# Interleaving the groups of an MLP's first layer with a lag of two parts

## The chip, the core and the metric

The kernel runs on one core of a Trainium2 chip. The metric is device time in microseconds for one execution, the median of several runs. Five engines work side by side: TensorE (PE in the profile) does the matmuls into PSUM banks, VectorE (DVE) and ScalarE (ACT) do elementwise work and empty PSUM, GpSimd (POOL) does elementwise work on SBUF, and SyncE (SP) issues the DMAs. Each engine executes its own list of instructions in order, and a wait at the head of the list holds everything behind it.

## The reference

Eight batches of x (100 rows of 512 numbers) attend to a context of 361 rows. A first plain cross-attention adds alpha times its result to x. Two multi-head cross-attentions with 16 heads of width 128 follow, each behind a layer norm and with biases and one extra bias key. The last stage is an MLP, and it is the only stage that the change touches:

```python
h = _layer_norm(x, ln_mlp_scale, ln_mlp_offset)
h = jax.nn.gelu(h @ w_fc1 + b_fc1, approximate=False) @ w_fc2 + b_fc2
return x + h
```

w_fc1 is 512 by 2048 and w_fc2 is 2048 by 512. Everything is float32.

## The kernel before

The MLP runs twice, for the batches 0 to 3 (half 0) and 4 to 7 (half 1). In each half the transposed activations are four chunks of 128 features by 400 rows. Both layers multiply with a fast scheme on 2 by 2 blocks that needs seven block products in place of eight, at the price of sums of blocks made beforehand.

The first layer of a half is cut into four groups, k = 0 to 3, of 512 hidden features each. `hidden_sums` (L1027) forms the sums of a group's weight blocks with four additions on POOL (helper `left_sums`, L1007 to L1010). `hidden_in` (L1016) forms the sums of the activations on DVE (helper `right_sums`, L1001 to L1004), once per half. `hidden` (L1034) then does a group in four parts, each with two products but the last, which has one:

- part 0: product gx (A11·B11), copied by ACT to c11 (L1058); product gy (A12·B21), added to c11 by DVE (L1059); gelu on ACT (L1055).
- part 1: product gz (S1·T1), copied by ACT to c22 (L1062); product S2·T2 added onto gx, copied by ACT to c12 (L1063).
- part 2: S4·B22 added onto gz, which DVE adds to c12 (L1065), and gelu; S3·T3 added onto gx, which DVE adds to c22 (L1067), and gelu.
- part 3: A22·T4 added onto gx, gelu straight from PSUM to c21; then the four `right_sums` of the group on DVE, which the second layer reads.

gx and gz gather several products in one PSUM bank each. A product that adds onto such a bank can't start before the engine that read the bank's earlier content is done. So the second product of part 1 waits for the copy of c11, part 2 waits for the copies of part 1, and part 3 waits for DVE's addition to c22.

The second layer follows: `mlp_sums` (L1074) forms the sums of w_fc2's blocks with four additions on DVE, and `mlp_out` (L1082) does its products (pfx, pfy, pfz in the profile). Both layers' weights are loaded by SP in pieces of 512 KB into a ring of six slots (class `Ring`, L51). Each group of the first layer holds two slots. A load into a slot is written behind the last unit that uses the slot's earlier content: group 3 takes the slots of group 0, and the second layer's first four pieces take those of groups 1 and 2. The sums of a group lie in a buffer of two turns (tag pT), so those of group k+2 wait for the last use of group k's, which is in its part 2.

`mlp_units` (L1238) returns the lists of units. The list `hid` of the first layer is written in the order: sums 0, hidden_in, then group after group, with the sums of the next group between parts 1 and 2 of a group. At the end (L1373) the kernel writes hid for half 0, then the second layer woven with the norm of half 1, then hid of half 1 woven with the final transposes and stores of half 0 (list `end`), then the second layer of half 1.

The order written is not yet the order of each engine's list. When the program is built, a planner goes through time with durations of its own and gives an engine that it takes to be free the first instruction, by the order written, that it takes to be ready. The trace shows the lists that came out of it.

Of the kernel before, what the change touches and what calls it, by code (L numbers as in the profile page):

```python
# [80 lines left out]
def two_cross_attentions(ctx: ExitStack, tc: tile.TileContext, a: dict, out: bass.AP):  # L81
# [11 lines left out]
    def psum(pool, shape, name):  # L93
        return pool.tile(shape, F32, tag=pool.name, name=name)
# [110 lines left out]
    def unit(fn, *keys):  # L205
        return fn, keys
# [360 lines left out]
    def normed(n, q, c):  # L567
        if c == 0:
            if n < 2:
                hTs[n, q] = work.tile([P, DT, NQ], F32, tag="hT", name=f"hT_{n}_{q}", bufs=1)  # L570
            elif q % 2 == 0:
                t = cpool.tile([P, 7 * 2 * KH], F32, tag="cT", name=f"hT_{n}_{q}")
                t = t[:, : DT * 2 * NQ].rearrange("p (c n) -> p c n", c=DT)
                for i in range(2):
                    hTs[n, q + i] = t[:, :, i * NQ : (i + 1) * NQ]
                hTs["mlp", q // 2] = t
            for j in range(QB):
                b = q * QB + j
                h = hTs["rows", j] = xs.pop(b)
                nc.vector.tensor_scalar(h, h, mv[:, b, 0:1], rstd[:, b : b + 1], ALU.subtract, ALU.mult)  # L580
        pt = psum(ps_t, [P, NQ], f"ph_{n}_{q}_{c}")
        for j in range(QB):
            nc.tensor.transpose(
                pt[:, j * L : (j + 1) * L], hTs["rows", j][:, c * P : (c + 1) * P], ident[:L, :L]
            )
        nc.vector.tensor_scalar(
            hTs[n, q][:, c, :], pt, vec_b[:, 2 * n, c : c + 1], vec_b[:, 2 * n + 1, c : c + 1], ALU.mult, ALU.add
        )
# [107 lines left out]
    pTs, probs, sums = {}, {}, {}  # L696
# [303 lines left out]
    def right_sums(engine, b11, b12, b21, b22, t1, t2, t4):  # L1000
        engine.tensor_tensor(t1, b12, b11, ALU.subtract)  # L1001
        engine.tensor_tensor(t2, b22, t1, ALU.subtract)
        engine.tensor_tensor(b12, b12, b22, ALU.subtract)
        engine.tensor_tensor(t4, b21, t2, ALU.subtract)  # L1004
# [7 lines left out]
    def blocks_of(t, n):  # L1012

        return [t[:, i * n : (i + 1) * n, j * NQ : (j + 1) * NQ] for i in range(2) for j in range(2)]

    def hidden_in(hf):  # L1016
        h = blocks_of(hTs["mlp", hf], 2)
        t = work.tile([P, 3, 2, NQ], F32, tag="pb", name=f"ht_{hf}", bufs=1)
        right_sums(nc.vector, *h, t[:, 0], t[:, 1], t[:, 2])
        ts["h", hf] = dict(zip(("B11", "T3", "B21", "B22", "T1", "T2", "T4"), h + [t[:, i] for i in range(3)]))  # L1020
        g0, g1 = (of[:, i * 3200 : (i + 1) * 3200].rearrange("p (f t) -> p f t", f=8) for i in range(2))
        t = zf[:, 6400:11200].rearrange("p (u f t) -> p u f t", u=3, f=8)
        g = [x[:, :, j * NQ : (j + 1) * NQ] for x in (g0, g1) for j in range(2)]
        gs[hf] = g
        ts["g", hf] = dict(zip(("B11", "T3", "B21", "B22", "T1", "T2", "T4"), g + [t[:, i] for i in range(3)]))

    def hidden_sums(hf, k):  # L1027
        w1, w2 = w4(("f1", hf, k)), w4(("f1", hf, 4 + k))
        t = work.tile([P, 3, 2, 256], F32, tag="pT", name=f"fs_{hf}_{k}")
        blocks = [w1[:, :2], w1[:, 2:], w2[:, :2], w2[:, 2:]]  # L1030
        left_sums(nc.gpsimd, *blocks, t[:, 0], t[:, 1], t[:, 2])
        ws["h", hf, k] = dict(zip(("A11", "A12", "S3", "A22", "S1", "S2", "S4"), blocks + [t[:, i] for i in range(3)]))

    def hidden(hf, k, part):  # L1034

        a, b = ws["h", hf, k], ts["h", hf]
        c11, c12, c21, c22 = (g[:, 2 * k : 2 * k + 2, :] for g in gs[hf])
        key = "h", hf, k

        def add(name, sa, sb, first=False):  # L1040
            if first:
                mm[key, name] = psum(ps_mm, [P, 2, NQ], f"p{name}_{hf}_{k}")
            ps = mm[key, name]
            for f in range(2):
                for c in range(2):
                    nc.tensor.matmul(  # L1046
                        ps[:, f, :], a[sa][:, c, f * P : (f + 1) * P], b[sb][:, c, :],
                        start=first and f == c == 0, stop=f == c == 1, skip_group_check=True,
                    )
            return ps  # L1050

        def gelu(dst, src, block):
            for f in range(2):
                i = block * 8 + 2 * k + f
                nc.scalar.activation(dst[:, f, :], src[:, f, :], AF.Gelu, bias=vec["b_fc1"][:, i : i + 1])  # L1055

        if part == 0:
            nc.scalar.copy(c11, add("gx", "A11", "B11", True))  # L1058
            nc.vector.tensor_tensor(c11, add("gy", "A12", "B21", True), c11, ALU.add)  # L1059
            gelu(c11, c11, 0)  # L1060
        elif part == 1:
            nc.scalar.copy(c22, add("gz", "S1", "T1", True))  # L1062
            nc.scalar.copy(c12, add("gx", "S2", "T2"))  # L1063
        elif part == 2:
            nc.vector.tensor_tensor(c12, add("gz", "S4", "B22"), c12, ALU.add)  # L1065
            gelu(c12, c12, 0)
            nc.vector.tensor_tensor(c22, add("gx", "S3", "T3"), c22, ALU.add)  # L1067
            gelu(c22, c22, 1)
        else:
            gelu(c21, add("gx", "A22", "T4"), 1)  # L1070
            t = [ts["g", hf][n][:, 2 * k : 2 * k + 2, :] for n in ("T1", "T2", "T4")]
            right_sums(nc.vector, c11, c12, c21, c22, *t)

    def mlp_sums(hf, c):  # L1074
        blocks = [w8(("f2", hf, cc, half)) for cc in (c, c + 2) for half in range(2)]
        t = cpool.tile([P, 20 * P], F32, tag="ctx", name=f"fs1_{hf}_{c}")
        t = t[:, :2048].rearrange("p (u f n) -> p u f n", u=2, f=8)
        s4 = work.tile([P, 8, P], F32, tag="pT", name=f"fs4_{hf}_{c}")
        left_sums(nc.vector, *blocks, t[:, 0], t[:, 1], s4)
        ws["o", hf, c] = dict(zip(("A11", "A12", "S3", "A22", "S1", "S2", "S4"), blocks + [t[:, 0], t[:, 1], s4]))  # L1080
# [119 lines left out]
    def rows_unit(q, tag="h"):  # L1200

        return unit(lambda: [load_rows(q * QB + j, tag=tag) for j in range(QB)])
# [35 lines left out]
    def mlp_units(hf):  # L1238
        norm = []
        for q in (2 * hf, 2 * hf + 1):  # L1240
            norm.append(rows_unit(q, "sums"))
            norm += [unit(lambda q=q, c=c: normed(2, q, c)) for c in range(DT)]
        hid, mlp = [unit(lambda: hidden_in(hf))], []
        for k in range(4):
            keys = [(W, ("f1", hf, k)), (W, ("f1", hf, 4 + k))]
            sums = unit(lambda k=k: hidden_sums(hf, k), *keys)
            hid.insert(len(hid) - 2 if k else 0, sums)
            hid += [unit(lambda k=k, part=part: hidden(hf, k, part), *keys) for part in range(4)]
        for c in range(2):
            a11, a12, a21, a22 = ((W, ("f2", hf, cc, half)) for cc in (c, c + 2) for half in range(2))  # L1250
            mlp.insert(len(mlp) - 1 if c else 0, unit(lambda c=c: mlp_sums(hf, c), a11, a12, a21, a22))
            for part, keys in enumerate(((a11, a12), (), (a21,), (a22,))):
                mlp.append(unit(lambda c=c, part=part: mlp_out(hf, c, part), *keys))
        def ends(j, chunks=range(DT)):
            return unit(lambda: back(ys["mlp", hf], j * L, hf * 4 + j, store, chunks))

        def fetch(*js):
            return unit(lambda: [load_rows(hf * 4 + j, "h" if j < 2 else "sums") for j in js])

        end = [fetch(2, 3), ends(2), ends(3), fetch(0, 1)]  # L1260
        end += [ends(j, cs) for cs in (range(3), range(3, 4)) for j in range(2)]
        return norm, hid, mlp, end
# [49 lines left out]
    for n, (l, q, g) in enumerate(steps):  # L1312
        ahead = project_units(n + 1) if n + 1 < len(steps) else []
        half_ahead = (len(ahead) + 1) // 2
        for j in range(QB):
            fill = []
            k = 2 * g + j
# [6 lines left out]
            part = ahead[:half_ahead] if j == 0 else ahead[half_ahead:]  # L1324
# [7 lines left out]
            part = woven(part, outs) if len(part) > len(outs) else woven(outs, part)  # L1332
            if mix:
# [3 lines left out]
                part = part[lead:]  # L1337
# [17 lines left out]
            lists, k = [], 0  # L1355
            for i, us in enumerate(groups):
                upto = (i + 1) * len(fill) // len(groups)
                lists += [us] + [[u] for u in fill[k:upto]]
                k = upto
            units += apart(lists)  # L1360
    n = len(steps) - 1
    drain = mix_units(n, 1) + [probs_unit(n)] + out_units(n)[1:] + close_units(1, 1)
    norm, hid, mlp, end = mlp_units(0)
    norm1, hid1, mlp1, end1 = mlp_units(1)
    units += held[8:] + norm[:5] + woven(drain, norm[5:])

# [33 lines left out]
```

## Time and profile before

| | us |
|---|---|
| median of 3 runs | 2000.42 (1997.58 to 2003.01) |
| the profiled execution | 2003.46 |
| its span, first to last instruction | 2001.6 |
| PE busy in the span | 1956.1 (98%) |
| DVE busy | 1278.3 (64%) |
| ACT busy | 755.1 (38%) |
| POOL busy | 703.7 (35%) |

PE's clock was granted at 0.999 of full speed over the span. In the trace the first layer of half 0 runs from about 1833 us to 1877 us, the second from there to 1912 us; half 1 follows to about 1960 us and to the end. In the stage of half 0's first layer (1833 to 1877 us) PE was busy 41.29 of 44.00 us, in that of half 1 (1912 to 1960 us) 47.15 of 48.00 us. A float32 matmul appears as two records on PE; one product of the first layer is eight records, and each of them takes about 0.17 us from start to start.

### The profile page before, as it was taken

What the parts mean: (1) busy time and instruction counts of PE and PEld (TensorE: products, weight loads), DVE (VectorE), ACT (ScalarE), POOL (GpSimd) and SP (SyncE); (2) the same over time, 40 slices, a digit from 0 to 9 for tenths busy, and PEclk for the clock granted to TensorE, in tenths of its full rate; (3) what the DMA queues carried; (4) which work ended last, traced back from release to release, by engine and by line L of the source; (5) the groups of instructions that cost most, each with busy time, mean ns of one, the idle gap of its engine ahead of it and who ended that gap; (6) DMA issues with size and microseconds to landing.
All of it is one profiled execution on the core that took longest, in us unless ns stands there. A gap on an engine that the chain in (4) does not pass through costs nothing.

```text
span 2001.6 us, 31490 instructions
## 1 busy us (share of the span) xinstructions
PE 1956.1 (98%) x10991; PEld 1810.4 (90%) x10991; DVE 1278.3 (64%) x3523; ACT 755.1 (38%) x2002; POOL 703.7 (35%) x1147
## 2 busy tenths in 40 slices
PE   9999999999999999999999999999999999999998
PEld 5668899999999899999999899999999999889998
DVE  2564776667677676676765756676767666765543
ACT  1324544344442344344433344444433444321231
POOL 3233433543344144434242323333243243225140
PEclk9999999999999999999999999999999999999999
DMA  7696324742645357616543453234334433135442
GB/s 254 248 318 208 95 83 125 233 137 66 192 155 163 107 143 236 192 54 188 171 128 115 129 172 99 85 88 159 92 123 126 144 119 87 45 97 180 124 126 70
DMA packets 250682, 283.89 MB, mean 142 GB/s; under 512 B 37608, under 2 KB 212108, under 8 KB 247196
## 3 DMA queue, kind: packets, MB, share of 16 engines
q1 hardware_dynamic: 246340, 271.51, 43.5%
q0 software_dynamic: 2112, 6.40, 0.9%
q10 hardware_dynamic: 2072, 3.97, 0.6%
q8 instruction: 88, 1.44, 0.3%
q14 instruction: 70, 0.57, 0.1%
HBM read 242.86 MB, written 38.97 MB: 141 GB/s over the span
## 4 chain that ended last, share of the span: by engine, by line
PE 80%; DVE 11%; ACT 4%; DMA 3%; issue 1%; POOL 0%; DVEq 0%; SPq 0%; ACTq 0%
PE sx L732 10%; PE mx L842 9%; PE pq L672 8%; PE pwo_P L955 7%; PE po L892 7%; PE mz L842 7%; PE pqw L688 7%; PE sz L732 5%; DVE pT L359 5%; PE my L842 3%; PE sy L732 2%; PE sc L479 2%; PE pfx L1095 2%; DMA xr<-xd 1%; PE pgx L1046 1%
## 5 line engine op out<-in xcount | busy, mean ns | idle before, releaser
L359 DVE STREAM_TRANSPOSE pT<-p 32x192 f32<-32x192 f32 (+1 forms) x1664 | 602.2, 362 | 89.0 <-ACT p L343 59.3
L842 PE MATMUL mx<-pT,ctx 128*128 128x256 f32 (+3 forms) x960 | 280.2, 391 | 9.2 <-DVE Z L868 3.8
L732 PE MATMUL sx<-cT,Z 128*128 128x181 f32 x1152 | 225.7, 317 | 2.1 <-DVE p L772 2.1
L766 POOL TENSOR_SCALAR p<-nsb 128x1 f32<-128x1 f32 x192 | 37.7, 216 | 499.3 <-DVE pT L359 448.4
L842 PE MATMUL mz<-pT,ctx 105*128 105x256 f32 (+3 forms) x768 | 206.1, 390 | 6.1 <-ACT Z L854 4.2
L732 PEld LDWEIGHTS sx<-cT,Z 128*128 128x128 f32 x1152 | 193.1, 190 | 13.7 <-DVE p L772 3.8
L672 PE MATMUL pq<-hT,wq 128*128 128x200 f32 x1024 | 194.2, 334 | 2.2 <-DMA wq<-in_L_xattn_wq_dram 2.2
L688 PE MATMUL pqw<-q,wkT 128*128 128x200 f32 x1024 | 193.9, 332 | 0.0
L842 PEld LDWEIGHTS mx<-pT,ctx 128*128 128x128 f32 (+1 forms) x960 | 169.4, 189 | 26.2 <-DVE Z L868 7.2
L892 PE MATMUL po<-Z,wv 128*128 128x200 f32 x1024 | 192.9, 332 | 0.0
L786 ACT ACTIVATE p<-p,nm 128x362 f32<-128x362 f32 x192 | 114.7, 597 | 181.0 <-DVE nm L785 170.3
L672 PEld LDWEIGHTS pq<-hT,wq 128*128 128x128 f32 x1024 | 177.4, 191 | 6.1 <-issue 2.5
L688 PEld LDWEIGHTS pqw<-q,wkT 128*128 128x128 f32 x1024 | 176.5, 189 | 5.4
L842 PEld LDWEIGHTS mz<-pT,ctx 128*128 128x128 f32 (+1 forms) x768 | 144.3, 190 | 38.6 <-ACT Z L854 8.8
L892 PEld LDWEIGHTS po<-Z,wv 128*128 128x128 f32 x1024 | 175.2, 189 | 3.5
L785 DVE TENSOR_REDUCE nm<-p 128x1 f32<-128x362 f32 x192 | 101.5, 529 | 112.7 <-ACT p L777 100.8
L691 ACT COPY Z<-pqw 128x400 f32<-128x400 f32 x256 | 122.3, 489 | 75.2 <-PE pqw L688 75.0
L732 PE MATMUL sz<-cT,sums 128*128 128x181 f32 x768 | 149.3, 316 | 0.7 <-ACT p L760 0.7
L715 POOL TENSOR_TENSOR sums<-Z 128x256 f32<-128x256 f32 x96 | 70.8, 737 | 215.4 <-ACT Z L691 135.5
L343 ACT ACTIVATE p<-p,rden 128x362 f32<-128x362 f32 (+2 forms) x216 | 129.1, 599 | 36.4 <-DVE rden L342 36.4
L732 PEld LDWEIGHTS sz<-cT,sums 128*128 128x128 f32 x768 | 124.7, 189 | 1.0 <-ACT p L760 1.0
L842 PE MATMUL my<-pT,ctx 128*128 128x256 f32 (+3 forms) x384 | 102.6, 388 | 0.0
(380 smaller groups left out, 3117.8 us busy)
## 6 DMA issues: line engine op xcount, KB each, us to landing
wv<-in_L_xattn_wv_dram SPq DMA_DIRECT2D x64, 512.0 KB
wq<-in_L_xattn_wq_dram SPq DMA_DIRECT2D x64, 512.0 KB
wkT<-wkd SPq DMA_DIRECT2D x48, 512.0 KB
cT<-cTd SPq DMA_DIRECT2D x16, 1267.0 KB
wo_S<-wod SPq DMA_DIRECT2D x32, 512.0 KB
f<-in_L_xattn_w_fc_dram SPq DMA_DIRECT2D x32, 512.0 KB
wo_A<-in_L_xattn_wo_dram SPq DMA_DIRECT2D x24, 512.0 KB
xr<-xd SPq DMA_DIRECT2D x45, 200.0 KB
```

The lines of the kernel that those rows point to most:

```text
L343: nc.scalar.mul(p[:rows, :n], p[:rows, :n], rden[:rows])
L359: nc.vector.transpose(dst[keys, :, :, i, :], src[i * QD : (i + 1) * QD, :, :, quarter, :])
L672: nc.tensor.matmul(ps, w[:, c, (h % 2) * K : (h % 2 + 1) * K], hTs[l, q][:, c, :], start=(c == 0), stop=(c == DT - 1),)
L688: nc.tensor.matmul(ps[:, c, :], w[:, h % 2, cc * P : (cc + 1) * P], qs[h], start=True, stop=True)
L691: nc.scalar.copy(Z[:, 2 * c2 : 2 * c2 + 2, :, h * L : (h + 1) * L], ps.rearrange("p c (b t) -> p c b t", b=QB),)
L715: nc.gpsimd.tensor_tensor(t[:, 0], a2[:, :2, :], a2[:, 2:, :], ALU.add)
L732: nc.tensor.matmul(ps[:, :KH], st["a"][a][:, c, :], st["ct"][:, blk, c, :], start=(first and c == 0), stop=(c == 1), skip_group_check=not ...
L785: nc.vector.tensor_reduce(nm, p[:, :S1], AX.X, ALU.max, negate=True)
L786: nc.scalar.activation(p[:, :S1], p[:, :S1], AF.Exp, bias=nm, accum_out=den)
L842: nc.tensor.matmul(ps, cx[:w, blk, :], pT[:w, u, :], start=first, stop=last, skip_group_check=more)
L892: nc.tensor.matmul(ps, w[:, c, (h % 2) * K : (h % 2 + 1) * K], Z[:, c, :, h * L : (h + 1) * L], start=(c == 0), stop=(c == DT - 1),)
L955: nc.tensor.matmul(ps, w[:, h, :], OB[i, j][:, h, :], start=(h == 0 and not more), stop=(h == 7), skip_group_check=more)
```

## The change

The list hid is written in another order. A group's parts 0 and 1 stand between the parts 2 and 3 of the group in front of it, and the sums of group k+2 stand behind part 2 of group k. Nothing is added or taken away: the same units with the same instructions.

```diff
-        hid, mlp = [unit(lambda: hidden_in(hf))], []
+        hid, mlp = [], []
         for k in range(4):
             keys = [(W, ("f1", hf, k)), (W, ("f1", hf, 4 + k))]
             sums = unit(lambda k=k: hidden_sums(hf, k), *keys)
-            hid.insert(len(hid) - 2 if k else 0, sums)
-            hid += [unit(lambda k=k, part=part: hidden(hf, k, part), *keys) for part in range(4)]
+            hid.append([sums] + [unit(lambda k=k, part=part: hidden(hf, k, part), *keys) for part in range(4)])
+
+        sums, parts = [us[0] for us in hid], [us[1:] for us in hid]
+        hid = [sums[0], unit(lambda: hidden_in(hf)), parts[0][0], sums[1], parts[0][1]]
+        for k in range(1, 5):
+            for i in range(2):
+                hid += parts[k][i : i + 1] if k < 4 else []
+                hid.append(parts[k - 1][2 + i])
+                if i == 0 and k < 3:
+                    hid.append(sums[k + 1])
```

With s for sums, "in" for hidden_in and two digits for group and part, the two orders are:

```
before: s0 in 00 01 s1 02 03 10 11 s2 12 13 20 21 s3 22 23 30 31 32 33
after:  s0 in 00 s1 01 10 02 s2 11 03 20 12 s3 21 13 30 22 31 23 32 33
```

## The prediction

> **What bounds the kernel now.** I read the page's first part, then busy time by stage, then PE's waits in the first-layer stages, then the timelines of PE, DVE and ACT at each wait.
>
> The page's busy line says that PE does work in 1956.1 of 2001.6 us:
>
> ```profile
> span 2001.6 us, 31490 instructions
> PE 1956.1 (98%) x10991; PEld 1810.4 (90%) x10991; DVE 1278.3 (64%) x3523; ACT 755.1 (38%) x2002; POOL 703.7 (35%) x1147
> ```
>
> The change leaves every instruction in place, so all it can win is idle time of PE in the two first-layer stages. The table by stage (the columns are PE, weight load, DVE, ACT, POOL, clock, DMA share, GB/s) gives that budget; its first and third rows are the two stages:
>
> ```profile
> 1833.00:1877.00 44.00, 41.29 (x240) 39.59 (x239) 29.82 (x52) 17.94 (x44) 16.00 (x14) 1.00 0.44 133
> ...
> 1912.00:1960.00 48.00, 47.15 (x282) 45.78 (x281) 30.32 (x42) 18.72 (x46) 14.13 (x11) 1.00 0.46 139
> ```
>
> 44.00 − 41.29 = 2.71 and 48.00 − 47.15 = 0.85 us: 3.56 us, or 0.18% of the kernel, is the most that can be won. The waits of PE between 1831 and 1960 us say what they are for:
>
> ```profile
> PE pgx L1046 <- DVE O L1067: 1.4, 3, 0.6
> PE pgx L1046 <- ACT O L1063: 1.4, 1, 1.4
> PE pgz L1046 <- ACT O L1062: 0.7, 2, 0.5
> ```
>
> These are the bank dependences inside a group: a product that adds onto gx or gz waits for the engine that read the bank. The timeline has six places. Two lie at a border of groups, 0.53 us at 1861.25 and 0.20 us at 1941.58. One is the last product of group 0 in half 0 (0.16 us at 1849.29). Two are the last products of group 3, at 1875.28 (0.60) and 1956.19 (0.62). The sixth wait, 1.37 us at 1846.49, is at the start of half 0.
>
> The first border wait in half 0, on ACT and then DVE:
>
> ```profile
> 1859.92 0.81 ACT L1055 ACTIVATE O<-O,vecs 128x200 f32<-128x200 f32 x2 [2.44 <-DVE O L1059]
> 1860.64 0.47 ACT L1062 COPY O<-pgz 128x400 f32<-128x400 f32 x1
> ```
>
> The copy of c22, which PE needs, stands behind a gelu that waits for DVE's addition to c11; on DVE that stood behind `right_sums` of the group in front, of which three took 1.29, 1.46 and 1.66 us instead of 0.57 while POOL worked on weight sums (1852.68 to 1858.48). So PE has too little other work between a bank's product and the next one onto it.
>
> At the end of a half, PE and DVE:
>
> ```profile
> 1873.51 1.18 PE L1095 MATMUL pfx<-O,f 128*128 128x200 f32 x6
> 1875.28 1.62 PE L1046 MATMUL pgx<-ht,f 128*128 128x200 f32 x8 [0.60 <-DVE O L1067]
> ...
> 1870.64 1.23 DVE L1007 TENSOR_TENSOR fs<-f,f 128x1024 f32<-128x1024 f32 x1 [1.70 <-DMA f<-in_L_xattn_w_fc_dram]
> 1871.90 1.22 DVE L1008 TENSOR_TENSOR fs<-fs,f 128x1024 f32<-128x1024 f32 x1
> 1873.05 1.22 DVE L1010 TENSOR_TENSOR f<-f,f 128x1024 f32<-128x1024 f32 x1
> 1874.18 0.57 DVE L1065 TENSOR_TENSOR O<-pgz,O 128x400 f32<-128x400 f32 x1
> 1874.66 0.56 DVE L1067 TENSOR_TENSOR O<-pgx,O 128x400 f32<-128x400 f32 x1
> ```
>
> The planner put three of `mlp_sums`' four additions ahead of group 3's additions to c12 and c22 (L1065, L1067). L1007 waited 1.70 us for a load, L1065 came at 1874.18 though its product ended near 1872.3, and the last product of group 3 came 0.60 us late in spite of six records of the second layer put in as a filler.
>
> **The change, part by part.** I count in products (eight records, 1.355 us: 1869.45 to 1870.80 to 1872.15). A half has 28.
>
> *The borders.* In the new order every product onto a gathered bank, group 3's last part excepted, has one to four products of another group between it and the one before on its bank. The least is two products for part 3 behind part 2 (2.71 us), against a latency of 0.57 us of DVE and some 0.1 us on either side. For part 2 behind part 1 there are again two, 2.71 us, where the copies cost 0.49 each. The 0.53, 0.20 and 0.16 go: −0.89 us. If the ACT list keeps a gelu ahead of a copy, the cover is 2.71 less the gelus' 0.81 or 0.82, still enough; without that cover the 0.89 comes back.
>
> *The loads.* All are on SP's queue, and their numbers and sizes stay. Part 3 of group 0 moves from product 7 to product 11 (its end), so the second half of group 3's weights is issued 5.4 us later. From issue to landing took 4.0 us in the one case that shows itself (1866.60 to 1870.64). It lands at product 14, and group 3's sums then take POOL four times 1.27 us, up to 1.6 where DVE holds it up: S1 at 15, all by 18. S1·T1 of group 3 is due at product 22. Hidden by 7 products, 9.5 us. The other sums have more. Behind these loads on SP stand row loads that nobody waits for in this stage. Part 3 of group 1 goes from 14 to 18, and the second layer's piece behind it still has ten products: hidden.
>
> *The last load, and DVE's list.* Part 3 of group 2 goes from product 21 to 25. Call its end T (1866.5 before). The fourth piece of w_fc2 is issued at T+0.1 and lands at T+4.1. Before, group 3's addition to c12 was due at T+5.7 and that to c22 at T+7.0. After, only part 2 of group 3 lies behind T: they are due at T+1.4 and T+2.7, and the last product, with the filler of six records (1.0 us), at T+3.7. Three orders of DVE's list are possible, and no row of before tells which the planner will take:
> (a) the additions stand ahead of `mlp_sums`: c22 is done at T+3.4, PE doesn't wait, and both waits of 0.60 and 0.62 are won: −1.22. S1 then stands behind `right_sums` of group 3. Its last product ends at T+5.1, gelu 0.75 and one sum 0.57 put `mlp_sums` at T+6.5 and S1 at T+7.7; pfz, which needs S1, is due at T+9.5. Hidden by 1.8 us.
> (b) one addition of `mlp_sums` is ahead of c22's: T+4.1 + 1.22 + 0.57 = T+5.9 for a product due at T+3.7, a wait of 2.2 where 0.6 was: +1.6 a half, +3.2.
> (c) three are ahead of both, as before: T+4.1 + 3 × 1.22 + 0.5 + 0.5 = T+8.7, a wait of 5.0: +4.4 a half, +8.8.
> The rows of before place the planner's landing: the third addition was put ahead of an instruction due at T+5.7, so it took L1007 to start by about T+3.3. Group 3's c22 is due before that now, at T+2.7, so (a) is nearest, with (b) close. I take (a).
>
> Here the Trainium skill speaks against the row. The page "DMA: Bandwidth & Descriptors", section "Anatomy of one DMA", gives about 2.0 us fixed and bytes over 436 GB/s, fitted on the software queue: an estimate of 2.0 + 1.2 = 3.2 us for 512 KB. The row has 4.0 us on SP's hardware queue, with other loads in flight. By the page's figure the waits in (b) and (c) shrink by 0.8 us a half, (b) to +1.6 in all and (c) to +7.2. The row decides.
>
> The same row of POOL beside DVE bears on the new order. The page "SBUF — State Buffer", section on two separate sides, says that a DVE operation with two SBUF inputs and a POOL operation exclude each other for a whole instruction. By that, three sums could lose up to 1.27 each, 3.8 us; the row lost 0.72 + 0.89 + 1.09 = 2.7. In the new order the sums of group 2 run in products 7 to 11, ahead of `right_sums` of group 0 (after 11), and those of group 3 in 14 to 18, ahead of `right_sums` of group 1 (after 18). The collision mostly goes, and PE was not waiting for it but at the border counted already: 0 either way.
>
> *The start of half 0.* The 1.37 us comes from two row normalisations (L580) of half 1 that the planner pulled forward on DVE and that waited for loads (1.10 and 1.68 us); behind them stood c11's addition, ACT's gelu and the copy of c12 (L1063). The change moves none of these. Before the copy, both orders hold eight products that PE may do, if S1·T1 of group 1 goes ahead of S3·T3 of group 0; if not, PE waits one product longer. I take 0, with ends −1.4 and +1.4.
>
> *The sum* against the profiled 2003.46 (span 2001.6 and 1.9 around it): −0.89 − 1.22 = −2.1, to 2001.3. That execution is 3.0 above the median of 2000.42. From the median the forecast is 1998.3.
>
> **The rivals.** A measurement of this kernel tells about 0.3% (6 us) from no change.
>
> 1. *mlp_sums blocks DVE at the end of both halves*, case (c): −0.9 + 8.8 = +7.9, 2008.3. For it: the planner did just this before, with three additions, and believed in an early load. Against it: the additions are now due 4.3 us sooner after T, so it would have to take the load to land in about a microsecond. It decides for slower once the two waits together grow by about 7 us, 3.5 us a half, which is two or more additions ahead with c12's also behind. A head that loses 1.4 would lower this point. Chance 0.32, with other late lists of the same kind counted in.
> 2. *One addition slips ahead*, case (b): −0.9 + 3.2 = +2.3, 2002.7. Chance 0.16.
> 3. *The change doesn't do what it says.* The planner already moves products (1862.68: part 2's product with six records of the next group's gx behind it, in one row of 14), so its lists may come out much alike, and the waits stay or reappear on the next bank: 0, 2000.4. Chance 0.12.
> 4. *Faster by over 6 us.* The budget of 3.56 us excludes it by this mechanism; left is a measurement that is off. Chance 0.07.
>
> **How the numbers follow.** The forecast has 0.33, and its own range is 1996 to 2001: the whole budget of 3.56 us below the median is 1996.9, the head's loss above the forecast 1999.7, with about a microsecond for the median. Slower by over 0.3% is rival 1, 0.32; faster is rival 4, 0.07; within is the rest, 0.33 + 0.16 + 0.12 = 0.61. The range for 8 in 10 takes in the forecast, rivals 2 and 3 and rival 1 to its computed 2008.3 and a little, 1996 to 2009; left out are rival 4 and about a third of rival 1, 0.07 + 0.11.
>
> **What would show it.** The waits of PE for ACT's copies L1062 should be gone, and those for L1067 at the last product of group 3 too; the first-layer stages' PE idle should fall from 3.56 us to about 1.5. On DVE, L1065 and L1067 of group 3 should stand ahead of L1007's wait for the load. If L1007 stands ahead of them, rivals 1 or 2 hold, and the wait at the last product gives the size. `right_sums` above 1 us should be rarer. The prediction would be wrong if a load of group 3's weights or a free PSUM bank is late, which would show as PE waiting at part 0 or 1 of a group.

## The result and the profile after

The changed kernel takes 1998.34 us (median of 14 runs, 1994.05 to 2001.70) against 1999.86 us before (14 runs, 1997.58 to 2003.04). The ratio is 0.9984 with a 95% interval of 0.9978 to 0.9991: 3.2 us faster, or 1.8 to 4.4. The two medians alone lie 1.5 us apart. A second, later comparison gave 0.9988 (0.9979 to 0.9998), 2.4 us, with medians 3.3 us apart. So the gain is real and its size known only roughly, as 1.5 to 3.3 us, inside the 0.3% (6 us) that the prediction counts as no change. The forecast was 2.1 us faster.

The profiled span fell by more, from 2001.6 to 1996.3 us. Most of that is not the change:

```profile
span 1996.3 us, 31478 instructions
PE 1952.8 (98%) x10991; PEld 1808.8 (91%) x10991; DVE 1277.8 (64%) x3523; ACT 757.1 (38%) x2002; POOL 704.4 (35%) x1147
```

The first product of half 0's first layer starts at 1830.19 us instead of 1833.65. Up to there the lists of all engines are the same, so 3.46 of the 5.3 us are chance. Over the 13 profiles of the table below it starts between 1830.0 and 1837.8 us. From that product to the last PE row the kernel takes 161.31 us instead of 163.09, 1.78 less. This stretch is what the experiments are read by.

PE's waits between 1831 and 1965 us, after:

```profile
PE pgx L1046 <- ACT O L1063: 2.0, 1, 2.0
PE pgx L1046 <- DVE O L1067: 0.8, 2, 0.6
```

The line for ACT's copy of c22 (L1062, 0.7 us in two waits) is gone, as forecast. The wait at the start of half 0 (the first line) grew from 1.37 to 2.04 us. The end of half 0 still waits, as DVE's timeline and then PE's show:

```profile
1864.30 1.23 DVE L1007 TENSOR_TENSOR fs<-f,f 128x1024 f32<-128x1024 f32 x1 [0.47 <-DMA f<-in_L_xattn_w_fc_dram]
...
1867.55 1.22 DVE L1010 TENSOR_TENSOR f<-f,f 128x1024 f32<-128x1024 f32 x1
1868.68 0.57 DVE L1004 TENSOR_TENSOR Z<-O,Z 128x400 f32<-128x400 f32 x1
1869.17 0.57 DVE L1065 TENSOR_TENSOR O<-pgz,O 128x400 f32<-128x400 f32 x1
1869.65 1.22 DVE L1009 TENSOR_TENSOR fs<-f,fs 128x1024 f32<-128x1024 f32 x1
1870.79 0.57 DVE L1067 TENSOR_TENSOR O<-pgx,O 128x400 f32<-128x400 f32 x1
```

```profile
1871.41 1.62 PE L1046 MATMUL pgx<-ht,f 128*128 128x200 f32 x8 [0.55 <-DVE O L1067]
```

All four additions of `mlp_sums` (L1007 to L1010; L1008 is in the rows left out) stand ahead of group 3's addition to c22, and three of them ahead of that to c12 (L1065), too. But L1007 ran at 1864.30, before the last product of group 2 (which ended at 1866.6). Its load did not wait for that product at all. In the prediction's count it should have landed 4.1 us behind it. SP's issues of the two pieces concerned, after:

```profile
1860.11 0.37 SPq L157 DMA_DIRECT2D f<-in_L_xattn_w_fc_dram  x1
1866.83 0.37 SPq L157 DMA_DIRECT2D f<-in_L_xattn_w_fc_dram  x1
```

The fourth piece of w_fc2 is issued at 1860.11, when group 3's gy has ended (1859.87), and the piece behind it goes at 1866.83, behind part 3 of group 2. By these times a slot of the ring is given out in the order in which slots come free, not by the place that it had. The trace before has the same: group 3's second piece of weights was issued as follows, right behind group 1's gy (its end was at 1843.61) and 5.4 us before part 3 of group 0 began (1849.29).

```profile
1843.85 0.39 SPq L157 DMA_DIRECT2D f<-in_L_xattn_w_fc_dram  x1
```

So the account of the slots in the section on the kernel before does not hold: group 3's second piece did not wait for the slot that group 0 gave up last.

### The profile page after: what moved, and what is told of

Same layout as the page of the kernel before. It is cut to its first block, busy times and chain, and to the rows that moved or that the text cites. A ratio compares the mean times of both kernels' runs of the same rounds, so it can differ in the third digit from the quotient of the medians.

```text
span 1996.3 us, 31478 instructions
## 1 busy us (share of the span) xinstructions
PE 1952.8 (98%) x10991; PEld 1808.8 (91%) x10991; DVE 1277.8 (64%) x3523; ACT 757.1 (38%) x2002; POOL 704.4 (35%) x1147
## 4 chain that ended last, share of the span: by engine, by line
PE 78%; DVE 9%; DMA 5%; ACT 3%; issue 2%; POOL 2%; SPq 1%; DVEq 0%; POOLq 0%; ACTq 0%
PE sx L732 10%; PE mx L842 9%; PE pq L672 8%; PE pwo_P L955 7%; PE po L892 7%; PE mz L842 7%; PE pqw L688 7%; DVE pT L359 5%; PE sz L732 5%; PE my L842 4%; PE sy L732 2%; DMA cxd<-msum 2%; PE pfx L1095 2%; PE sc L479 2%; PE pgx L1046 1%
```

## The experiments

I read each profile in three figures, all on PE: the gaps in the first 18 us of the stretch (the start of half 0), in the rest of half 0's first layer, and in half 1's first layer. A gap is the start of a row less the start of the row ahead of it and less its records' time (0.169 us each; 0.085 and 0.108 for the two kinds of transpose). Each line is one profile; the ratios are from many runs.

| kernel | start | half 0 | half 1 | stretch, us | ratio to before |
|---|---|---|---|---|---|
| before | 2.53 | 1.62 | 1.48 | 163.09 | |
| changed | 2.59 | 0.81 | 0.48 | 161.31 | 0.9984 |
| changed, again | 1.30 | 0.37 | 0.18 | 159.24 | 0.9988 (0.9979 to 0.9998) |
| new order in half 0 only | 1.31 | 0.48 | 1.67 | 160.89 | 0.9998 (0.9989 to 1.0007) |
| new order in half 1 only | 1.53 | 1.34 | 0.18 | 160.50 | 0.9994 (0.9987 to 1.0001) |
| group 3 late | 0.20 | 0.71 | 0.69 | 159.06 | 0.9989 (0.9982 to 0.9996) |
| lag of one part | 1.25 | 2.05 | 1.48 | 162.23 | 0.9997 (0.9990 to 1.0004) |
| old, few POOL sums | 0.76 | 0.60 | 1.82 | 160.63 | one run, 2001.46 us |
| new, sums pinned | 0.18 | −0.01 | 0.15 | 157.78 | 0.9984 (0.9977 to 0.9992) |
| new, rows pinned | 0.17 | 0.47 | 0.18 | 158.28 | 0.9987 (0.9978 to 0.9997) |
| new, both pinned | 0.18 | −0.02 | 0.15 | 158.33 | 0.9976 (0.9967 to 0.9986) |
| new, both pinned, again | 0.18 | −0.01 | 0.16 | 158.32 | 0.9982 (0.9972 to 0.9992) |
| old, both pinned | 1.25 | 0.73 | 0.73 | 160.78 | 0.9993 (0.9985 to 1.0002) |

**One half at a time.** The order is the new one in one half only:

```diff
+        if hf != 0:   # 1 in the other kernel
+            hid = <the order before>
```

> The new order in half 0 only, the old one in half 1. I read the stretch from the first product of half 0's first layer to the last PE row: 163.09 us before, 161.31 us after the change; in it, half 0 up to its first pfz product 47.67 and 46.91, half 1 from the row at its second gx piece to its first pfz product 46.31 and 45.31. If the gain is the lag between products on one bank, it is made in each half by itself: half 0 reads 46.9, half 1 46.3, the stretch 162.3. If it comes from where weights and sums of one half stand for the other, or is a run-to-run matter, one half moves without its own order being changed, or neither does.

> The new order in half 1 only. The lag in each half by itself gives half 0 47.7, half 1 45.3, stretch 162.1. The rival of a run-to-run matter gives no such split.

In the measure of the expectations, half 0 read 45.30 and half 1 46.50 us in the first kernel, 46.39 and 45.01 in the second. Half 1 follows its own order: in the table, 1.48 and 1.67 us of gaps with the old one, 0.48, 0.18 and 0.18 with the new. Half 0 was missed by 1.6 and 1.3 us; 1.28 and 1.00 of that are in the start (2.59 to 1.31, 2.53 to 1.53), which differs between profiles with the same list of instructions. Behind the start, half 0 has 1.62 and 1.34 with the old order and 0.81, 0.48 and 0.37 with the new. So each half gains by itself; by the means, 1.48 − 0.55 = 0.9 us in half 0 and 1.58 − 0.28 = 1.3 us in half 1, 2.2 us in all. The times of the two kernels don't resolve halves of that.

**Group 3 behind group 2's end.**

```diff
-  ... s3 21 13 30 22 31 23 32 33
+  ... s3 21 13 22 23 30 31 32 33
```

> The new order, but group 3 starts behind part 3 of group 2, in both halves: the lag stays in groups 0 to 2 and goes from the border of groups 2 and 3. The load of the fourth piece of w_fc2 then goes back behind the last product of group 2, as before the change. If the gain is from the borders of the earlier groups, half 0 stays near 46.9 (its end waits 0.55 to 0.65 in either order) and half 1 near 45.7, the end wait going from 0.21 back to about 0.6. If the early load is what won, both halves go back to 47.7 and 46.3.

There is no wait at a border, and the ends wait 0.45 and 0.42. SP's list shows the load going back, and DVE what it does, in this kernel:

```profile
1862.46 0.37 SPq L157 DMA_DIRECT2D f<-in_L_xattn_w_fc_dram  x1
```

```profile
1866.37 1.23 DVE L1007 TENSOR_TENSOR fs<-f,f 128x1024 f32<-128x1024 f32 x1 [1.56 <-DMA f<-in_L_xattn_w_fc_dram]
```

The last product of group 2 ends at 1862.27, the load goes at 1862.46 and lands 3.9 us later. So an earlier load is not what the borders gain by: they gain here without it. It may be worth something at the end: this kernel's ends cost 0.6 us of gaps each, those of the new order 0.46 (0.72, 0.40, 0.27) in half 0 and 0.12 (0.37, 0, 0) in half 1. In half 0 the three profiles spread around 0.6, so only half 1 shows it. In the measure of the expectation half 1 read 45.52, near the 45.7, and half 0 read 44.42, since its start had only 0.20 us of gaps.

**A lag of one part.**

```diff
-  00 s1 01 10 02 s2 11 03 20 12 s3 21 13 30 22 31 23 32 33
+  00 01 s1 02 10 03 11 s2 12 20 13 21 s3 22 30 23 31 32 33
```

> A lag of one part: 00 01 02 10 03 11 12 20 13 21 22 30 23 31 32 33, with the sums where the buffers allow. Part 3 still has two products between it and its part 2, part 2 only one or none on its bank. If one part of lag is enough for ACT and DVE to catch up (latency 0.5 to 0.6 us against one product of 1.36 us), the halves read 46.9 and 45.3 as with two. If the wait at the border comes from ACT's list holding the copy of c22 behind a gelu, part of 0.53 and 0.20 comes back: 47.2 and 45.5.

The wait at the border came back whole, and larger: 0.69 and 0.35 us. ACT, DVE and PE of this kernel:

```profile
1858.11 0.81 ACT L1055 ACTIVATE O<-O,vecs 128x200 f32<-128x200 f32 x2 [3.61 <-DVE O L1059]
1858.83 0.72 ACT L1055 ACTIVATE O<-pgx,vecs 128x200 f32<-128x200 f32 x2
1859.45 0.48 ACT L1062 COPY O<-pgz 128x400 f32<-128x400 f32 x1
```

```profile
1855.92 1.67 DVE L1003 TENSOR_TENSOR O<-O 128x400 f32<-128x400 f32 x1
1857.51 0.56 DVE L1059 TENSOR_TENSOR O<-pgy,O 128x400 f32<-128x400 f32 x1
```

```profile
1860.08 1.59 PE L1046 MATMUL pgz<-hT,fs 128*128 128x200 f32 x8 [0.69 <-ACT O L1062]
```

The copy of c22 stands behind two gelus, the first of which waits 3.61 us for the addition to c11; that stands behind three slow `right_sums`. Not the latency of one copy (0.49 us) but the list ahead of it decides, and one product (1.36 us) doesn't cover it. In this order part 2 of group 2 follows directly on its part 1 ("21 s3 22"), as in the old one, so at the place of the wait the distance is the old one. Half 1 read 46.31, as before the change and above both guesses (45.3 and 45.5). Half 0 read 46.81, below both, only because its start had 1.25 us of gaps and not 2.59.

**POOL's sums taken away from the old order.**

```diff
-        left_sums(nc.gpsimd, *blocks, t[:, 0], t[:, 1], t[:, 2])
+        if k < 2:
+            left_sums(nc.gpsimd, *blocks, t[:, 0], t[:, 1], t[:, 2])
+        else:
+            ...  # three memsets of 16 columns; S1, S2 and S4 are raw blocks
```

> The old order with the POOL sums of groups 2 and 3 left out in both halves: their products multiply raw weight blocks in place of the sums, so the output is another; the number of products is the same. If POOL's hold on DVE made the two border waits (three right_sums at 1.3 to 1.7 us instead of 0.57, then c11, gelu and the copy of c22 late), right_sums go to 0.57 and the border waits of 0.53 and 0.20 go: half 0 47.1, half 1 46.1. If the distance between the products alone made them, they stay: 47.7 and 46.3.

`right_sums` of group 1 fell to 0.57 us and both border waits went, in the old order (ACT's gelu is L1061 in this kernel):

```profile
1853.19 0.57 DVE L1001 TENSOR_TENSOR Z<-O 128x400 f32<-128x400 f32 x1
1854.15 0.57 DVE L1002 TENSOR_TENSOR Z<-O,Z 128x400 f32<-128x400 f32 x1 [0.40 <-ACT O L1061]
```

So POOL's hold on DVE is what makes the border waits (one profile; both waits went), and distance between the products is what covers it. The new order doesn't avoid the hold. In the changed kernel `right_sums` of group 1 are as slow as before, and PE goes on into part 2 of group 2 with no wait, behind three products of other groups (4.1 us):

```profile
1853.79 1.28 DVE L1001 TENSOR_TENSOR Z<-O 128x400 f32<-128x400 f32 x1
1855.17 1.46 DVE L1002 TENSOR_TENSOR Z<-O,Z 128x400 f32<-128x400 f32 x1
1856.56 1.65 DVE L1003 TENSOR_TENSOR O<-O 128x400 f32<-128x400 f32 x1
...
1859.87 1.52 PE L1046 MATMUL pgz<-hT,fs 128*128 128x200 f32 x8
```

Half 0 read 44.87 for want of a wait at its start, too. Half 1 read 46.65 and not 46.1: its end waited 1.39 us, since L1007 waited 2.12 us for the load, against 1.35 before.

**The two waits that are left.** The first addition of `mlp_sums` is pinned on DVE behind what is written before it, and the two row normalisations (L580) that DVE takes in the first 10 us of the stretch are pinned to the second layer, where they are written:

```diff
-        engine.tensor_tensor(s1, a21, a22, ALU.add)
+        pin(engine.tensor_tensor(s1, a21, a22, ALU.add))   # mlp_sums only
```

```diff
-                nc.vector.tensor_scalar(h, h, mv[...], rstd[...], ALU.subtract, ALU.mult)
+                ins = nc.vector.tensor_scalar(h, h, mv[...], rstd[...], ALU.subtract, ALU.mult)
+                if (n, q) == (2, 2):
+                    tc.keep_in_program_order(ins)
```

> The new order with the first addition of mlp_sums pinned behind everything written before it on DVE. If mlp_sums ahead of group 3's additions makes the end waits of 0.55 and 0.21, both go and the stretch falls from 161.3 to 160.6. If S1 then comes late, PE waits at the first pfz instead, by up to 1 us, and nothing is won.

> The new order with the two row normalisations of half 1 that DVE takes at the start of half 0 pinned to where they are written, in the second layer. If they make the wait of 2.04 us at the start of half 0, it goes: half 0 reads 44.9 and the stretch 159.3. The rival is that the copy of c12 waits for something else behind it (the table load of gelu, 1.28 us on ACT), and 0.5 to 1 us of the wait stays.

> Both pins on the new order. If the two waits add up: stretch 158.5, 2.8 us below the change and 4.6 below before, a ratio to before of about 0.997 (the change alone measured 0.9984). If they overlap, less.

With the sums pinned, both ends are free and no pfz waits. This is the list of the prediction's case (a). At the end of half 0 DVE has:

```profile
1871.75 0.57 DVE L1067 TENSOR_TENSOR O<-pgx,O 128x400 f32<-128x400 f32 x1 [0.78 <-PE pgx L1046]
...
1875.38 1.22 DVE L1007 TENSOR_TENSOR fs<-f,f 128x1024 f32<-128x1024 f32 x1
```

S1 is done at 1876.60, and the first pfz product starts at 1878.49: 1.9 us of cover, where the prediction counted 1.8.

With the rows pinned, the start has no wait, though the table load of gelu is still there, so that load alone doesn't make it (half 0 read 45.06 for the expected 44.9; stretch 158.28 for 159.3, the ends not waiting in this profile). That the normalisations make it is not shown by this kernel: in two of the profiles with the old place (group 3 late, and the kernel above, whose stretch of 157.78 is the shortest) the start had no wait either. The two pins together cost about 0.5 us at the transposes of the rows, which now come late (gaps between the first layers of 1.03 to 1.11 us with both pins, 0.43 to 0.49 in all other kernels; with the rows alone pinned, 0.19 of the 0.47 us counted to half 0 are of this kind). Both pins together read 158.33, near the expected 158.5. In time they gave 0.9976, then again:

> The changed kernel itself once more, beside its variants on one chip and with a second profile. Ratio 0.998 to 0.999. If the wait at the start of half 0 is chance in the landing of the row loads, it differs from the first profile's 2.04 us with every instruction the same, and the second of the two row normalisations moves with it; if it belongs to the order, it is 2 us again.

> Both pins on the new order, a second time, beside the changed kernel. It read a ratio of 0.9976 to before. From the gaps of PE it should be 0.76 us (the two end waits) plus the mean of the start's wait (0.6 us over eight profiles) less 0.5 us for the transposes of the rows that now come late: 0.8 us or 0.04% below the changed kernel, within the interval of the comparison. If it is 0.1% below again, something outside these gaps counts.

> Both pins on the old order. If the change's gain is in the border waits alone, the end waits (0.60 and 0.62) and the start's wait go here without it, and what is left against the new order with the pins is the border waits of 0.53 and 0.20 and the short gaps between split products: half 1 reads 44.6 us against 43.86. If the pins do all that the change did, half 1 reads 43.9.

Side by side, the changed kernel has 0.9988 and the one with both pins 0.9982, intervals that overlap. The pins are at best a few hundredths of a per cent; I would not call them a gain on this. The start of the changed kernel had 0.14 us of gap where its first profile had 2.20, and a wait of 0.62 us at part 3 of group 0 in its place. The second normalisation, in the first and in the second profile of the same kernel:

```profile
1840.48 1.18 DVE L580 TENSOR_SCALAR xr<-xr,mv,rstd 100x512 f32<-100x512 f32 x1 [2.83 <-DMA xr<-xd]
```

```profile
1841.54 0.55 DVE L580 TENSOR_SCALAR xr<-xr,mv,rstd 100x512 f32<-100x512 f32 x1 [1.53 <-DMA xr<-xd]
```

Counted from the stretch's start, DVE got to it at 10.3 us in the one and 8.9 us in the other, and in the first it also took 1.18 us, with POOL at work on weight sums. This wait is chance. With the old order and both pins half 1 read 44.44 (expected 44.6): the border waits stay there, at 0.51 in half 0 and 0.19 us in half 1. The pins do not replace the lag.

## Why the prediction was right, and where it was not

The total and the cause at the borders came as forecast. At the ends the size came out near the forecast by luck: two steps were wrong, and their errors worked against each other.

*The borders: right, with a term too small.* The 0.53 and 0.20 us are in each half that has the old order and POOL's sums (0.53 and 0.20 in the kernels with one half changed, too, 0.51 and 0.19 with both pins), and in none with the new. But each costs more than its row says: the gap is 0.70 for 0.53, 0.37 for 0.20. They were worth 1.07 us instead of 0.73. The cause is the one that was read from the lists; taking POOL's sums away showed it.

*The 0.16 us at part 3 of group 0: wrong as a term.* It is gone in the first profile of the changed kernel, but the wait did not go with the order: it was 0.51 in the kernel with the new order in half 0 and 0.62 in the second profile of the changed kernel. It follows how long DVE takes for the first of `right_sums` of group 0 (L1001), which stands ahead of the addition to c22. In the second profile of the changed kernel:

```profile
1845.32 1.57 DVE L1001 TENSOR_TENSOR Z<-O 128x400 f32<-128x400 f32 x1 [0.44 <-ACT O L1055]
1846.82 0.56 DVE L1067 TENSOR_TENSOR O<-pgx,O 128x400 f32<-128x400 f32 x1
```

In the old order 0.78, 0.91 and 1.06 us of L1001 go with waits of 0.16, 0.29 and 0.51; in the new 0.79, 1.47 and 1.57 go with 0, 0.51 and 0.62. In the six profiles with 0.57 or 0.58 there is no wait. So the new order covers here some 0.2 to 0.4 us, by two more records (0.34 us) ahead of part 3, and the rest is DVE's. PE's list has one product between the parts 2 and 3 of group 0, not the two that the prediction counted.

*The loads: wrong.* "The second half of group 3's weights is issued 5.4 us later" and "the fourth piece of w_fc2 is issued at T+0.1 and lands at T+4.1" took each load to wait for the slot in its own turn. Group 3's second half was issued 10.2 us into the stretch before and 9.6 after. For the fourth piece, the slot that came free first was that of group 3's first weights, behind its gy, which the new order brings ahead of group 2's part 3. So the load is some 6.7 us earlier than counted, and case (c)'s 8.8 us could not come about by it. This was the ground of the main rival, whose chance of 0.32 rested on it.

*The ends: wrong list, near the size by luck.* The prediction took (a). The list of the changed kernel was that of (c): in both halves three additions of `mlp_sums` stand ahead of group 3's additions to c12 and c22, and in half 0 the fourth stands ahead of c22's. By its own count this would have cost 8.8 us. It did not, since the load came so much sooner and the additions were mostly done by then. So the sign "if L1007 stands ahead of them, rivals 1 or 2 hold" came up, and neither rival held. The ends fell from 0.62 us of gaps (0.75, 0.48) to 0.46 (0.72, 0.40, 0.27) in half 0, which is within the spread of the profiles, and from 0.88 (0.79, 0.96) to 0.12 (0.37, 0, 0) in half 1, which is clear of it. That is 0.92 us for the 1.22 of the sum.

*The collision of POOL and DVE: wrong step, same price.* `right_sums` of group 1 do not all stand behind product 18. Three of them need only part 2, and fall into group 3's sums as before. In the two first layers eight sums of a group took over 1 us before and eight after, so they did not become rarer. At the border of groups 1 and 2 that cost nothing, as said.

*The start: taken as 0, and not settled.* Its gaps are 2.53 and 1.53 us with the old order and 2.59, 1.31, 1.30, 0.20 and 0.18 with the new (the last two with group 3 late and with the sums pinned), so chance is as large as any difference. With the rows pinned, it is 1.25 in the one profile of the old order (0.67 of it at part 3 of group 0, where L1001 took 1.06 us) and 0.17 to 0.18 in three of the new. So the new order may gain something here, too, which the sum below leaves out.

*The budget: too small.* Idle time of 3.56 us is less than the gaps, which were 5.63 us in the two first layers before (2.53 + 1.62 + 1.48). By the prediction's measure of idle time, about 1.5 us should have been left. Over stages shifted with the start of the stretch it was 2.59 + 0.22 = 2.81 in the first profile of the changed kernel, where the wait at the start had grown, and 0.73 in the second.

Together 1.07 + 0.92, and about 0.2 in short gaps, are the 2.2 us of the gaps, beside a forecast of 2.1 whose terms were 0.89 and 1.22, and beside 2.4 and 3.2 us in the two comparisons, whose intervals hold it.

## What to carry to other kernels

When PE waits for a copy that is short, look at the list ahead of the copy on its engine, and ahead of what that waits for: the distance that the products need is set by the slowest run of that chain and not by the copy. Reordering for distance can cover a collision that stays. Before a load is costed by "its" buffer, look in the order of issues at what each one waited for, since an allocator that hands out what is free first can turn a later use into an earlier load; and repeat the profile before a single wait is put down to an order.

## What the hardware showed that was not expected

A wait of PE costs about 0.16 us more than the row's idle time: 0.70 for 0.53, 0.75 for 0.60, 0.37 for 0.20, 0.79 for 0.62, 2.20 for 2.04. The records themselves show why: one lasts 0.332 us, but the next starts 0.169 us behind it, and the idle time counts from the end of the last record, 0.163 us later than the next could have started. The first matmul behind each of the six waits of the kernel before takes longer besides, 408 to 437 ns against 332, and the second starts 0.24 to 0.27 us behind it. That is another 0.08 to 0.10 us, which shows in the gap of the next row. The products of part 3, two of them behind a wait (shortest, median and longest record in ns):

```profile
L1046 PE MATMUL pgx<-ht,f x32: 332/332/437, 1849.3 to 1876.6; 128*128 128x200 f32 x32
```

The start of the stretch, with nothing changed ahead of it, lay up to 7.7 us apart in 13 profiles. Behind it, a wait of 2.04 us came or went between two profiles of the same kernel, as the normalisation behind a 200 KB load ran 1.4 us later or sooner. Both are as large as the change.
